# Two transformer layers in f32 on one core: values and first queries/keys as seven block products, and another pacing of the filling work

## The chip, the cores and the metric

The kernel runs on one core of a Trainium2 chip, as one launch. The metric is the device time of the launch in microseconds, the median of several runs. All arithmetic is f32.

## The reference

Two layers, each with a normalisation, causal attention with 16 heads of 32, and a gated feed-forward branch beside it. Tokens: 2 batches of 1024, width 512.

```python
xn = _layernorm(x, axis=-1)
x = x + _L0_attn_ref(xn, Wq, Wk, Wv, Wo) + _L0_ffn_ref(xn, w_gate, w_up, w_down)
xn = _layernorm(x, axis=-1)
x = x + _L1_attn_ref(xn, ...) + _L1_ffn_ref(xn, ..., gate_s, up_s, down_s)
# attention: Q, K, V = xn @ W.T; rotary turn of Q and K; causal softmax(Q K / sqrt(32)) V; @ Wo.T
# feed-forward: (silu(xn @ gate.T) * (xn @ up.T)) @ down.T; hidden width 2048, then 1408
# (in layer 1 gate, up and down have a scale per output)
```

The change concerns `V = xn @ Wv.T` and the Q and K of the first four heads.

## The kernel before, in words

**Phases.** A phase is one layer for one batch: (0, 0), (0, 1), (1, 0), (1, 1). The normalised input is held transposed in `xnT[ph, 0]` and `xnT[ph, 1]`, the first and the second 512 tokens, each 128 partitions by 4 chunks of the width by 512 tokens. For seven-product forms `ln_sums` (L561) and `ln_last_sum` (L572) make sums of blocks of it (`xs`, three tiles, and the last one in place in `xnT[ph, 1]`) on POOL.

**Units.** A `Unit` (L591) multiplies two weight blocks with both halves of the input in seven products instead of eight (Winograd's form of Strassen's method): four methods, `first` (L664) to `fourth` (L698), with 4, 4, 4 and 2 matmuls of 512 columns; the running sums stay in two PSUM banks (x and y; a third bank z is short-lived). `needs` (L654) lists what a method reads, for the planner. `sums` (L614) and `more_sums` (L626) make the sums of weight blocks on POOL, one unit ahead; in the first batch of a layer they are stored in DRAM, in the second they are loaded. `Hidden` (L944) is the unit of one 128-wide slice of gate and up, `QueriesKeys` (L763) that of a group of four heads' queries and keys. The queries and keys of a phase's first group, however, are four plain projections by `project_qk` (L752), 4 matmuls each, and the values are four calls of `project_v` (L812), 8 matmuls each (a shared partial sum in place of full products).

**Steps.** The attention of a phase is 40 steps (4 groups of heads, each with query blocks of 1, 2, 3 and 4 steps). In a step the main loop (L1462 and after) issues the scores of one step, the softmax pieces of earlier ones, and, LAG = 5 steps later, `weighted` (the product with the values) and at a block's end `total` and `normalise`. Between scores and `weighted` a `Fill` (L1207) puts other matmuls: units from a list `main`, the down projections `downs` (with additions onto x by DVE), output projections `outs`, further units of queries and keys `qk` that are due at a step, `values`, and `timed` items (loads, statistics of the next normalisation, `scale_down`, L890, which scales layer 1's down weights into DRAM during phase 0). `choose` (L1299) takes the next item; where a planned wait of `main` exceeds a bound, it takes a down projection. How much goes into a step is set by

```python
share = fill.left((ph + 1) * per_phase) / (end - i)
goal = share + max(-4.0, min(4.0, carried))
```

(L1508), in units of one matmul of 512 columns: what is left in the phase over the steps that are left. The last phase has LAG steps more, without scores.

**The end of a phase.** `queue_phase` (L1354) puts the next phase's transposes (8 tiles, one after the other) at the end of `main`; `project_qk` stands after the transposes 4 (k, first half), 5 (q, first half) and 7 (k and q, second half), and the first hidden unit of the next phase after them. The next phase's scores start when all four are done.

**Order.** The program's instructions aren't issued as they are written: `Schedule` (L152 and after) records them with modelled costs. PE keeps its recorded order; the other engines' orders are chosen by due times in `again` (L340).

**Buffers that matter.** `tmp`, tag "xs": two buffers of 128 x 512, used for raw inputs of the normalisation and by `scale_down`. `t5_p`: four buffers for copies out of PSUM. Three PSUM banks serve all filling work.

Of the kernel before, what the change touches and what calls it, by code (L numbers as in the profile page):

```python
# [40 lines left out]
def ts(n, size):  # L41
    return slice(n * size, (n + 1) * size)
# [364 lines left out]
def two_layers(ctx: ExitStack, tc: tile.TileContext, x_in, attn_w, ffn_w, ffn_s, rope, out):  # L407
# [48 lines left out]
    def let_go(name):  # L456
        bank_held[bank_of.pop(name)] = False
# [131 lines left out]
        nc.sync.dma_start(out=w[:, 2:4, :], in_=src[D // 2 :, :].rearrange("(c p) e -> p c e", p=P))  # L589

    class Unit:  # L591

# [46 lines left out]
        def product(self, bank, a, b, start=False):  # L639
            for c in range(2):  # L640
# [6 lines left out]
                    skip_group_check=True,  # L647
                )

        def scale(self):  # L650

            return None

        def needs(self, kind):  # L654

            if kind == "second":
                return [self.one, self.s12]
            if kind == "third":
                return [self.u, self.p5, self.s4]
            if kind == "fourth":  # L660
                return [self.p5]
            return []

        def first(self):  # L664
            self.begin()
            a, _ = self.weights()
            x0 = xnT[self.ph, 0]
            self.x = bank(f"ux{self.name}", hold=True)
            self.product(self.x, a[:, 0:2], x0[:, 0:2], start=True)
            one = self.one = keep(self.x, f"p1{self.name}")  # L670
            z = bank(f"uz{self.name}")
            self.product(z, a[:, 2:4], x0[:, 2:4], start=True)
            self.c11(z, one)

        def second(self):
            t1, t2, _ = xs[self.ph]
            self.product(self.x, self.s12[:, 1], t2)
            self.u = keep(self.x, f"u{self.name}")
            self.y = bank(f"uy{self.name}", hold=True)
            self.product(self.y, self.s12[:, 0], t1, start=True)  # L680
            self.p5 = keep(self.y, f"p5{self.name}", self.scale())

        def third(self, nxt):
            _, b = self.weights()
            x1 = xnT[self.ph, 1]
            self.product(self.x, b[:, 0:2], x1[:, 0:2])
            if nxt:
                nxt.sums()
            if self.scale() is None:
                nc.vector.tensor_tensor(self.p5, self.x, self.p5, ALU.add)  # L690
            else:
                nc.vector.scalar_tensor_tensor(self.p5, self.x, self.scale(), self.p5, ALU.mult, ALU.add)
            self.c22(self.p5)
            self.product(self.y, self.s4, x1[:, 2:4])
            let_go(f"uy{self.name}")
            self.c12(self.y, self.u)

        def fourth(self, nxt):  # L698
            _, b = self.weights()
            self.product(self.x, b[:, 2:4], xs[self.ph][2])  # L700
            let_go(f"ux{self.name}")
            if nxt:
                nxt.more_sums()
            self.c21(self.x)

    def keep(bank, name, scale=None):
        t = t5_p.tile([P, TB], F32, tag="t5", name=name)
        if scale is None:
            nc.scalar.copy(t, bank)
        else:  # L710
            nc.scalar.activation(t, bank, AF.Copy, scale=scale)
        return t
# [50 lines left out]
    class QueriesKeys(Unit):  # L763
# [8 lines left out]
        def begin(self):  # L772
            pass
# [5 lines left out]
        def c22(self, k1):  # L779
            rotated(self.ph, self.g, "k", 1, k1)  # L780

        def c12(self, bank, u):
# [26 lines left out]
        wv[ph] = wv_p.tile([P, DC, D], F32, tag="wv", name=f"wv{ph}")  # L809
        nc.sync.dma_start(out=wv[ph], in_=attn_w[layer][2].rearrange("(c p) e -> p c e", p=P))  # L810

    def project_v(ph, t):  # L812


        x0, x1, t1 = xnT[ph, 0], xnT[ph, 1], xs[ph][0]
        cols = ts(t, P)

        def product(bank, a, c0, start):
            for c in range(2):
                nc.tensor.matmul(  # L820
                    bank,
                    a[:, c, cols],
                    wv[ph][:, c0 + c, :],
                    start=(start and c == 0),
                    stop=(c == 1),
                    skip_group_check=True,
                )

        ps0 = bank(f"ps_v{ph}_{t}", hold=True)
        product(ps0, x0[:, 0:2], 0, True)  # L830
        both = keep(ps0, f"vv{ph}_{t}")
        ps1 = bank(f"ps_w{ph}_{t}")
        product(ps1, t1, 0, True)
        product(ps1, x1[:, 2:4], 2, False)
        for n in (0, 4):
            v[ph, t + n] = xp.tile([P, D], F32, tag=f"v{t + n}", name=f"v{ph}_{t + n}")
        nc.vector.tensor_tensor(v[ph, t + 4], ps1, both, ALU.add)
        product(ps0, x0[:, 2:4], 2, False)
        let_go(f"ps_v{ph}_{t}")
        nc.scalar.copy(v[ph, t], ps0)  # L840
        if t == QC // 2 - 1 and ph + 1 < len(phases):
            load_wv(ph + 1)

    parts = {}

# [98 lines left out]
    class Hidden(Unit):  # L944
# [19 lines left out]
        def c11(self, bank, one):  # L964
            nc.vector.tensor_tensor(self.h[0], bank, one, ALU.add)

        def c22(self, up):
            self.up = up

        def c12(self, bank, u):  # L970
            nc.vector.tensor_tensor(self.h[1], bank, u, ALU.add)
# [235 lines left out]
    class Fill:  # L1207
# [2 lines left out]


        def __init__(self):
            self.timed, self.main, self.downs, self.outs, self.qk, self.values = [], [], [], [], [], []

            self.later = 0.0
            self.turn = False
            self.unit = None
# [15 lines left out]
            self.main[at:at] = items  # L1233

        def left(self, end):
            n = 8.0 * len(self.values) + sum(item[0] for item in self.main) + self.later
            n += sum(len(d[2]) for d in self.downs) + 14.0 * len(self.qk)
            return n + sum(1.0 for o in self.outs if o[0] < end)

# [39 lines left out]
                    return o  # L1279
            return None  # L1280

        def do_values(self):
            self.values.pop(0)[2]()
            self.turn = False
            return 8.0

        def do_output(self, o):
            self.outs.remove(o)
            output_alone(*o[1:])
# [64 lines left out]
    def queue_phase(ph):  # L1354
# [236 lines left out]
```

## Time and profile before

| what | value |
|---|---|
| median of 3 runs | 1867.2 us (1863.83 to 1868.71) |
| the profiled execution's own time | 1868.41 us |
| its span | 1866.6 us |
| mean granted clock of TensorE | 0.997 |
| ACT, POOL busy share | 56%, 63% |

Each line of a profile gives an engine and an instruction's group. PE is TensorE's matmuls, PEld its weight loads (which run beside), DVE VectorE, ACT ScalarE, POOL GpSimd, SP the queue of most DMAs. A group line names output and inputs, tile form and count, then busy time and the mean of one, then idle time before it and what ended it. All instructions have one line number, 265, that of the helper that issues them, so they are told apart by tile: `sc` scores, `av` the product with the values, `ux`, `uy`, `uz` the banks of units (`ux_qk` and so on those of queries and keys), `d` down and output projections, `ps_o` output projections alone, `ps_v`, `ps_w` the values, `ps_k`, `ps_q` the plain projections, `tr` transposes of the normalised input, `mtr` those of softmax maxima. A timeline line is start, length, engine, instruction and count; what stands in brackets is an idle time and its releaser. A line of a busy table is a stretch, then for PE, PEld, DVE, ACT and POOL busy time and instructions, the granted clock, and the DMA share and rate.

### The profile page before, as it was taken

What the parts mean: (1) busy time and instruction counts of PE and PEld (TensorE: products, weight loads), DVE (VectorE), ACT (ScalarE), POOL (GpSimd) and SP (SyncE); (2) the same over time, 40 slices, a digit from 0 to 9 for tenths busy, and PEclk for the clock granted to TensorE, in tenths of its full rate; (3) what the DMA queues carried; (4) which work ended last, traced back from release to release, by engine and by line L of the source; (5) the groups of instructions that cost most, each with busy time, mean ns of one, the idle gap of its engine ahead of it and who ended that gap; (6) DMA issues with size and microseconds to landing.
All of it is one profiled execution on the core that took longest, in us unless ns stands there. A gap on an engine that the chain in (4) does not pass through costs nothing.

```text
span 1866.6 us, 25444 instructions
## 1 busy us (share of the span) xinstructions
PE 1838.2 (98%) x9180; PEld 838.8 (45%) x9180; DVE 1408.2 (75%) x1958; ACT 1038.8 (56%) x1243; POOL 1179.8 (63%) x1124
## 2 busy tenths in 40 slices
PE   7999999999999999999999999999999999999997
PEld 3444444444444444444444444444444444444443
DVE  3577866758778577587587786978879887989787
ACT  3465554546557464445375645665665665666661
POOL 5575856756567355373356875878758766766664
PEclk9999999999999999999999999999999999999998
DMA  5544222222243222222223323222222312221111
GB/s 197 161 140 140 83 65 68 85 66 83 68 136 108 94 80 63 68 79 81 68 82 102 119 85 129 64 74 73 80 83 88 124 35 91 72 69 52 57 39 67
DMA packets 139726, 164.21 MB, mean 88 GB/s; under 512 B 13264, under 2 KB 93136, under 8 KB 139600
## 3 DMA queue, kind: packets, MB, share of 16 engines
q1 hardware_dynamic: 139600, 162.58, 27.5%
q8 instruction: 73, 1.20, 0.3%
q14 instruction: 53, 0.43, 0.1%
HBM read 134.23 MB, written 28.31 MB: 87 GB/s over the span
## 4 chain that ended last, share of the span: by engine, by line
PE 88%; DVE 5%; DMA 3%; POOL 2%; ACT 1%; issue 1%; SPq 0%; POOLq 0%; DVEq 0%; ACTq 0%
PE d L265 23%; PE ux L265 18%; PE uy L265 8%; PE av L265 8%; PE sc L265 8%; PE uz L265 4%; PE ux_qk L265 4%; PE ps_w L265 3%; PE ps_v L265 3%; DVE s L265 2%; PE uy_qk L265 2%; PE ps_k L265 2%; PE ps_o L265 1%; PE ps_q L265 1%; DMA mb<-md 1%
## 5 line engine op out<-in xcount | busy, mean ns | idle before, releaser
L265 DVE TENSOR_TENSOR s<-s,mb 128x1024 f32<-128x1024 f32 (+2 forms) x448 | 492.1, 1132 | 24.7 <-DMA mb<-md 24.7
L265 POOL TENSOR_TENSOR acc<-acc,s 128x512 f32<-128x512 f32 (+1 forms) x384 | 478.1, 1270 | 39.5 <-ACT s L265 38.0
L265 ACT ACTIVATE s<-s 128x1024 f32<-128x1024 f32 (+1 forms) x320 | 305.3, 971 | 182.0 <-DVE s L265 179.7
L265 DVE TRANSPOSE_TENSOR_REDUCE rmax<-s 128x32 f32<-128x1024 f32 (+1 forms) x320 | 350.9, 1118 | 72.5 <-POOL s L265 42.1
L265 PE MATMUL d<-wd,hT 128*128 128x512 f32 x864 | 401.0, 597 | 0.4 <-ACT xnT L265 0.2
L265 ACT ACTIVATE s<-sc 128x1024 f32<-128x1024 f32 (+1 forms) x320 | 282.9, 933 | 207.9 <-PE sc L265 204.0
L265 POOL TENSOR_TENSOR acc<-s 128x512 f32<-128x512 f32 (+1 forms) x128 | 153.6, 1214 | 235.4 <-PE av L265 173.2
L265 PEld LDWEIGHTS d<-wd,hT 128*128 128x128 f32 x864 | 162.8, 191 | 201.1 <-issue 187.3
L265 DVE TENSOR_TENSOR x<-d,x 128x512 f32<-128x512 f32 x224 | 151.7, 678 | 93.1 <-PE d L265 92.1
L265 ACT ACT_TABLE_LOAD x160 | 205.3, 1283 | 10.9 <-DVE s L265 8.1
L265 PE MATMUL av<-s,v 128*32 128x256 f32 (+1 forms) x2560 | 159.7, 365 | 3.0 <-ACT s L265 2.0
L265 PEld LDWEIGHTS av<-s,v 128*32 128x32 f32 x2560 | 66.9, 109 | 148.7 <-issue 105.0
L265 POOL TENSOR_SCALAR_AFFINE_SELECT s<-s 128x512 f32<-128x512 f32 x128 | 89.9, 716 | 66.6 <-ACT s L265 64.9
L265 POOL TENSOR_TENSOR hT<-p,hT 128x512 f32<-128x512 f32 x53 | 75.8, 1430 | 75.2 <-ACT hT L265 75.2
L265 PE MATMUL ux<-xs,wu 128*128 128x512 f32 x212 | 100.8, 598 | 3.1 <-DVE p L265 3.1
L265 PE MATMUL ux<-xnT,wu 128*128 128x512 f32 x212 | 101.5, 601 | 0.0
L265 PE MATMUL ux<-xs,ws 128*128 128x512 f32 x212 | 101.0, 599 | 0.0
L265 PE MATMUL ux<-xnT,wg 128*128 128x512 f32 x212 | 101.0, 599 | 0.0
L265 PE MATMUL uy<-xnT,ws 128*128 128x512 f32 x212 | 99.7, 593 | 0.0
L265 PE MATMUL uz<-xnT,wg 128*128 128x512 f32 x212 | 99.6, 592 | 0.0
L265 PE MATMUL uy<-xs,ws 128*128 128x512 f32 x212 | 99.6, 592 | 0.0
L265 PE MATMUL d<-wo,oT 128*128 128x512 f32 x192 | 99.3, 599 | 0.1
(158 smaller groups left out, 2412.7 us busy)
## 6 DMA issues: line engine op xcount, KB each, us to landing
mb<-md SPq DMA_DIRECT2D x64, 512.0 KB, 3.7
wg<-in_gate SPq DMA_DIRECT2D x54, 256.0 KB, 2.8
wd<-in_down SPq DMA_DIRECT2D x32, 256.0 KB, 3.0
xr<-xm SPq DMA_DIRECT2D x32, 256.0 KB, 3.1
wu<-in_up SPq DMA_DIRECT2D x28, 256.0 KB, 2.9
s12gu<-ws SPq DMA_DIRECT2D x26, 256.0 KB, 2.0
ws<-s12gu SPq DMA_DIRECT2D x26, 256.0 KB, 2.6
wd<-wds SPq DMA_DIRECT2D x22, 256.0 KB, 2.9
```

The lines of the kernel that those rows point to most:

```text
L265: target(*[get(a) for a in args], **{k: get(a) for k, a in kwargs.items()})
```

## The change

- `project_v` goes; a class `Values(Unit)` computes the values by the four methods of a unit. The weight is cut into quarters (halves of the contraction by halves of the outputs), and a unit covers two tiles of 128 tokens in each half of the input (`pair` 0 or 1), so a phase has two. A product is four matmuls of 256 columns into the two halves of a bank. Sums of quarters, shared by both units, are made on POOL: s1 and s2 in the two "xs" buffers, s4 in a buffer of its own, the fourth in place in the weight.
- The values become `qk` items that are due at steps 3 and 4 of a phase and don't begin before steps 4 and 5 (`begins`).
- The first queries and keys of phases 1 to 3 become a `QueriesKeys` unit after all eight transposes. Phase 0's stay as they were.
- `c22` does the addition onto `p5` itself (the same instruction as before for `Hidden` and `QueriesKeys`); `needs` lists the input's sums as well.
- `scale_down` moves from steps 4 to 14 to steps 9 to 17 of phase 0.
- A step's share is weighted: 1.2 in the first ten steps of a phase, 1.5 in the last six of the program, 1 elsewhere.

```diff
--- before.py
+++ after.py
...
+        def blocks(self):
+            a, b = self.weights()
+            return (a[:, 0:2], a[:, 2:4], b[:, 0:2], b[:, 2:4]), (self.s12[:, 0], self.s12[:, 1]), self.s4
...
         def needs(self, kind):
             if kind == "second":
-                return [self.one, self.s12]
+                return [self.one, *self.sums_in(), *xs[self.ph]]
             if kind == "third":
-                return [self.u, self.p5, self.s4]
+                return [self.u, self.p5, self.s4, xnT[self.ph, 1]]
...
         def first(self):
             self.begin()
-            a, _ = self.weights()
+            a11, a12 = self.first_blocks()
...
-            self.product(self.x, a[:, 0:2], x0[:, 0:2], start=True)
+            self.product(self.x, a11, x0[:, 0:2], start=True)
...
-            self.product(z, a[:, 2:4], x0[:, 2:4], start=True)
+            self.product(z, a12, x0[:, 2:4], start=True)
             self.c11(z, one)
...
         def second(self):
...
-            self.product(self.x, self.s12[:, 1], t2)
+            _, (s1, s2), _ = self.blocks()
+            self.product(self.x, s2, t2)
...
-            self.product(self.y, self.s12[:, 0], t1, start=True)
...
         def third(self, nxt):
-            _, b = self.weights()
+            (_, _, s3, _), _, s4 = self.blocks()
...
-            self.product(self.x, b[:, 0:2], x1[:, 0:2])
+            self.product(self.x, s3, x1[:, 0:2])
...
-            if self.scale() is None:
-                nc.vector.tensor_tensor(self.p5, self.x, self.p5, ALU.add)
-            else:
-                nc.vector.scalar_tensor_tensor(self.p5, self.x, self.scale(), self.p5, ALU.mult, ALU.add)
-            self.c22(self.p5)
-            self.product(self.y, self.s4, x1[:, 2:4])
+            self.c22(self.x, self.p5)
+            self.product(self.y, s4, x1[:, 2:4])
...
         def fourth(self, nxt):
-            _, b = self.weights()
-            self.product(self.x, b[:, 2:4], xs[self.ph][2])
+            (_, _, _, a22), _, _ = self.blocks()
+            self.product(self.x, a22, xs[self.ph][2])
...
@@ -809,37 +821,85 @@
...
-    def project_v(ph, t):
-
-
-        x0, x1, t1 = xnT[ph, 0], xnT[ph, 1], xs[ph][0]
...
-        ps0 = bank(f"ps_v{ph}_{t}", hold=True)
-        product(ps0, x0[:, 0:2], 0, True)
-        both = keep(ps0, f"vv{ph}_{t}")
-        ps1 = bank(f"ps_w{ph}_{t}")
-        product(ps1, t1, 0, True)
-        product(ps1, x1[:, 2:4], 2, False)
-        for n in (0, 4):
-            v[ph, t + n] = xp.tile([P, D], F32, tag=f"v{t + n}", name=f"v{ph}_{t + n}")
-        nc.vector.tensor_tensor(v[ph, t + 4], ps1, both, ALU.add)
-        product(ps0, x0[:, 2:4], 2, False)
-        let_go(f"ps_v{ph}_{t}")
-        nc.scalar.copy(v[ph, t], ps0)
-        if t == QC // 2 - 1 and ph + 1 < len(phases):
-            load_wv(ph + 1)
+    class Values(Unit):
...
+        HALF = D // 2
+        shared = {}
+        def __init__(self, ph, pair, begins):
+            self.ph, self.pair, self.name, self.begins = ph, pair, f"_v{ph}_{pair}", begins
+        def quarter(self, c, r):
+            return wv[self.ph][:, 2 * c : 2 * c + 2, r * self.HALF : (r + 1) * self.HALF]
+        def first_blocks(self):
+            return self.quarter(0, 0), self.quarter(1, 0)
+        def blocks(self):
+            s1, s2, s4 = self.shared[self.ph]
+            a = self.quarter(0, 0), self.quarter(1, 0), self.quarter(0, 1), self.quarter(1, 1)
+            return a, (s1, s2), s4
+        def sums(self):
+            if self.ph in self.shared:
+                return
+            a11, a21, a22 = self.quarter(0, 0), self.quarter(0, 1), self.quarter(1, 1)
+            s1, s2 = (tmp.tile([P, 2, self.HALF], F32, tag="xs", name=f"s{n}_v{self.ph}") for n in (1, 2))
+            s4 = ws_p.tile([P, 2, self.HALF], F32, tag="wv4", name=f"s4_v{self.ph}")
+            self.shared[self.ph] = s1, s2, s4
+            nc.gpsimd.tensor_tensor(s1, a21, a22, ALU.add)
+            nc.gpsimd.tensor_tensor(s2, s1, a11, ALU.subtract)
+        def sums_in(self):
+            return list(self.shared[self.ph][:2])
+        def more_sums(self):
+            s1, s2, self.s4 = self.shared[self.ph]
+            if self.pair == 0:
+                nc.gpsimd.tensor_tensor(self.s4, self.quarter(1, 0), s2, ALU.subtract)
+                a21 = self.quarter(0, 1)
+                nc.gpsimd.tensor_tensor(a21, self.quarter(0, 0), a21, ALU.subtract)
+        def product(self, bank, a, b, start=False):
+            for n in range(2):
+                for c in range(2):
+                    nc.tensor.matmul(
+                        bank[:, n * self.HALF : (n + 1) * self.HALF],
+                        b[:, c, ts(2 * self.pair + n, P)],
+                        a[:, c, :],
+                        start=(start and n == 0 and c == 0),
+                        stop=(c == 1),
+                        skip_group_check=True,
+                    )
+        def begin(self):
+            self.v = [xp.tile([P, 2, D], F32, tag=f"v{self.pair}{n}", name=f"v{self.ph}_{self.pair}{n}") for n in range(2)]
+        def part(self, n, r):
+            return self.v[n][:, :, r * self.HALF : (r + 1) * self.HALF]
+        def pair_of(self, t):
+            return t.rearrange("p (n e) -> p n e", n=2)
+        def c11(self, bank, one):
+            nc.vector.tensor_tensor(self.part(0, 0), self.pair_of(bank), self.pair_of(one), ALU.add)
+        def c22(self, bank, p5):
+            nc.vector.tensor_tensor(self.part(1, 1), self.pair_of(bank), self.pair_of(p5), ALU.add)
+        def c12(self, bank, u):
+            nc.vector.tensor_tensor(self.part(1, 0), self.pair_of(bank), self.pair_of(u), ALU.add)
+        def c21(self, bank):
+            nc.scalar.copy(self.part(0, 1), self.pair_of(bank))
+            for n in range(2):
+                for i in range(2):
+                    v[self.ph, 4 * n + 2 * self.pair + i] = self.v[n][:, i, :]
+            if self.pair == 1 and self.ph + 1 < len(phases):
+                load_wv(self.ph + 1)
...
@@ -964,8 +1024,12 @@
...
-        def c22(self, up):
+        def c22(self, bank, up):
             self.up = up
+            if self.scale() is None:
+                nc.vector.tensor_tensor(up, bank, up, ALU.add)
+            else:
+                nc.vector.scalar_tensor_tensor(up, bank, self.scale(), up, ALU.mult, ALU.add)
...
         def left(self, end):
-            n = 8.0 * len(self.values) + sum(item[0] for item in self.main) + self.later
+            n = sum(item[0] for item in self.main) + self.later
...
         def choose(self, step):
             main = self.main[0] if self.main else None
-            v = self.values[0] if self.values and self.values[0][0] <= step else None
-            if main and main[2] in ("third", "fourth"):
-                v = None
-            if v and v[1] <= step:
-                return self.do_values, 8.0
...
+            full = full or (main and main[2] == "first" and getattr(main[3], "begins", 0) > step)
...
-            if v:
-                return self.do_values, 8.0
...
-        for t in range(QC // 2):
-
-            fill.values.append((t0 + (4, 4, 5, 5)[t] if ph else 0, t0 + (4, 4, 6, 6)[t], lambda t=t: project_v(ph, t)))
+        for pair in range(2):
+            begins = t0 + 4 + pair
+            fill.qk.append((begins - 1, Values(ph, pair, begins)))
+        fill.qk.sort(key=lambda x: x[0])
         if ph == 0:
             for k in range(HIDDEN[1]):
-                fill.at(t0 + 4 + k, lambda k=k: scale_down(k))
+                fill.at(t0 + 9 + 3 * k // 4, lambda k=k: scale_down(k))
...
@@ -1419,9 +1474,8 @@
...
-            for w in {4: "k", 5: "q", 7: "kq"}.get(t, ""):
-                fill.add(PROJ, lambda w=w, half=t // 6: project_qk(nxt, w, half), "other", lambda half=t // 6: [xnT[nxt, half]])
         fill.add(0.0, lambda: (ln_last_sum(nxt), marks.append(nxt)))
+        fill.add_unit(QueriesKeys(nxt, 0, 0), slices[0])
         fill.add_unit(units[nxt, 0], slices[0] + 1)
...
@@ -1457,6 +1511,13 @@
...
     total = len(steps)
+    def weight(i):
+        if i >= total + LAG - 6:
+            return 1.5
+        return 1.2 if i % per_phase < 10 else 1.0
...
         end = total + LAG if ph == len(phases) - 1 else (ph + 1) * per_phase
-        share = fill.left((ph + 1) * per_phase) / (end - i)
+        share = fill.left((ph + 1) * per_phase) * weight(i) / sum(weight(j) for j in range(i, end))
```

More of the change, by code (lines that the diff above doesn't have):

```diff
@@ L591, in two_layers @@
     class Unit:
+        s4 = None
         def kept(self):
@@ L665, in first @@
             self.begin()
-            a, _ = self.weights()
+            a11, a12 = self.first_blocks()
             x0 = xnT[self.ph, 0]
             self.x = bank(f"ux{self.name}", hold=True)
-            self.product(self.x, a[:, 0:2], x0[:, 0:2], start=True)
+            self.product(self.x, a11, x0[:, 0:2], start=True)
             one = self.one = keep(self.x, f"p1{self.name}")
             z = bank(f"uz{self.name}")
-            self.product(z, a[:, 2:4], x0[:, 2:4], start=True)
+            self.product(z, a12, x0[:, 2:4], start=True)
             self.c11(z, one)
+        def first_blocks(self):
+            a, _ = self.weights()
+            return a[:, 0:2], a[:, 2:4]
+        def sums_in(self):
+            return [self.s12]
         def second(self):
             t1, t2, _ = xs[self.ph]
-            self.product(self.x, self.s12[:, 1], t2)
+            _, (s1, s2), _ = self.blocks()
+            self.product(self.x, s2, t2)
             self.u = keep(self.x, f"u{self.name}")
             self.y = bank(f"uy{self.name}", hold=True)
-            self.product(self.y, self.s12[:, 0], t1, start=True)
+            self.product(self.y, s1, t1, start=True)
             self.p5 = keep(self.y, f"p5{self.name}", self.scale())
         def third(self, nxt):
-            _, b = self.weights()
+            (_, _, s3, _), _, s4 = self.blocks()
             x1 = xnT[self.ph, 1]
-            self.product(self.x, b[:, 0:2], x1[:, 0:2])
+            self.product(self.x, s3, x1[:, 0:2])
             if nxt:
                 nxt.sums()
-            if self.scale() is None:
-                nc.vector.tensor_tensor(self.p5, self.x, self.p5, ALU.add)
-            else:
-                nc.vector.scalar_tensor_tensor(self.p5, self.x, self.scale(), self.p5, ALU.mult, ALU.add)
-            self.c22(self.p5)
-            self.product(self.y, self.s4, x1[:, 2:4])
+            self.c22(self.x, self.p5)
+            self.product(self.y, s4, x1[:, 2:4])
             let_go(f"uy{self.name}")
@@ L777, in c11, with c22 @@
             rotated(self.ph, self.g, "q", 0, one)
-        def c22(self, k1):
+        def c22(self, bank, k1):
+            nc.vector.tensor_tensor(k1, bank, k1, ALU.add)
             rotated(self.ph, self.g, "k", 1, k1)
@@ L810, in load_wv, with first_blocks, sums_in @@
         nc.sync.dma_start(out=wv[ph], in_=attn_w[layer][2].rearrange("(c p) e -> p c e", p=P))
-    def project_v(ph, t):
-        x0, x1, t1 = xnT[ph, 0], xnT[ph, 1], xs[ph][0]
[L816 to L827, printed above, removed]
-        ps0 = bank(f"ps_v{ph}_{t}", hold=True)
-        product(ps0, x0[:, 0:2], 0, True)
-        both = keep(ps0, f"vv{ph}_{t}")
-        ps1 = bank(f"ps_w{ph}_{t}")
-        product(ps1, t1, 0, True)
-        product(ps1, x1[:, 2:4], 2, False)
-        for n in (0, 4):
-            v[ph, t + n] = xp.tile([P, D], F32, tag=f"v{t + n}", name=f"v{ph}_{t + n}")
-        nc.vector.tensor_tensor(v[ph, t + 4], ps1, both, ALU.add)
-        product(ps0, x0[:, 2:4], 2, False)
-        let_go(f"ps_v{ph}_{t}")
-        nc.scalar.copy(v[ph, t], ps0)
-        if t == QC // 2 - 1 and ph + 1 < len(phases):
-            load_wv(ph + 1)
+    class Values(Unit):
[5 more added lines that the diff above has]
+            return wv[self.ph][:, 2 * c : 2 * c + 2, r * self.HALF : (r + 1) * self.HALF]
+        def first_blocks(self):
+            return self.quarter(0, 0), self.quarter(1, 0)
[12 more added lines that the diff above has]
+            nc.gpsimd.tensor_tensor(s2, s1, a11, ALU.subtract)
+        def sums_in(self):
+            return list(self.shared[self.ph][:2])
[35 more added lines that the diff above has]
+                load_wv(self.ph + 1)
@@ L1212, in __init__ @@
         def __init__(self):
-            self.timed, self.main, self.downs, self.outs, self.qk, self.values = [], [], [], [], [], []
+            self.timed, self.main, self.downs, self.outs, self.qk = [], [], [], [], []
             self.later = 0.0
@@ L1280, in late_output @@
             return None
[L1282 to L1285, printed above, removed]
         def do_output(self, o):
```

## The prediction

> **What bounds the kernel now.** I read the page first (engine totals, slices), then PE's groups by form, then PE's timeline at four places, PE's waits, and the busy table of the last phase. The page:
>
> ```profile
> span 1866.6 us, 25444 instructions
> PE 1838.2 (98%) x9180; PEld 838.8 (45%) x9180; DVE 1408.2 (75%) x1958; ACT 1038.8 (56%) x1243; POOL 1179.8 (63%) x1124
> PE   7999999999999999999999999999999999999997
> ```
>
> PE is busy in 98% of the span and falls below nine tenths only in the first and the last slice. DVE, next at 75%, has slack. So a matmul taken out should shorten the span by what it takes in the stream. The groups' mean (about 597 ns) is the length of one record with its pipeline; the stream's pace is the distance between starts. PE's timeline in phase 0 shows it (start, length, count):
>
> ```profile
> 52.04 1.88 PE L265 MATMUL ps_v<-wv,xnT 128*128 128x512 f32 x4
> 53.75 1.88 PE L265 MATMUL ps_w<-wv,xs 128*128 128x512 f32 x4
> 55.47 1.88 PE L265 MATMUL ps_w<-wv,xnT 128*128 128x512 f32 x4
> ```
>
> Four records take 53.75 - 52.04 = 1.71 us, 0.429 each. The groups show two records for each matmul of the code (`project_v` issues 4 + 4 matmuls in 16 calls, 128 in all):
>
> ```profile
> L265 PE MATMUL ps_v<-wv,xnT 128*128 128x512 f32 x128 | 60.9, 601 | 0.0
> L265 PE MATMUL ps_w<-wv,xs 128*128 128x512 f32 x64 | 30.2, 594 | 0.3 <-DVE p_qk L265 0.3
> L265 PE MATMUL ps_w<-wv,xnT 128*128 128x512 f32 x64 | 30.1, 592 | 0.0
> ```
>
> 128 + 64 + 64 = 256 records. A matmul of 512 columns is therefore 2 x 0.429 = 0.858 us of PE's time.
>
> **Values, on the path.** Before: 32 matmuls per phase, 27.5 us. After: two units of 7 products, each product 2 x 2 matmuls of 256 columns, 56 matmuls per phase, 112 records. No full-array record of 256 columns is in the trace. If it takes half of 0.429, the phase costs 112 x 0.2145 = 24.0 us: 3.43 us less, 13.7 us in four phases. The bounds: from below half, as a record streams its columns. From above, the question is whether a weight load per 256 columns stays hidden. The nearest rows are the transposes, a fresh load for every 128 columns, and a pair of loads of the f32 kind (PE, then PEld):
>
> ```profile
> 508.61 0.60 PE L265 MATMUL tr<-ident,xr 128*128 128x128 f32 x4
> 508.94 0.30 PEld L265 LDWEIGHTS ps_o<-wo,oT 128*128 128x128 f32 x2
> ```
>
> Four transposes in 0.60 us, one being 0.273 long (their group's mean, 277 ns), start (0.60 - 0.273) / 3 = 0.109 us apart, a quarter of 0.429: a load per 128 columns did not slow that stream. Two f32 loads of 0.19 each end within 0.30, so 0.11 apart. By the transposes a 256-column record is 0.218, which takes 448 x 0.0035 = 1.6 us off the gain. The upper end is a load that shows: a group of four right after scores is 1.98 long where one in the stream is 1.88 ("98.70 1.88" against "48.50 1.98" in the timeline), so 0.10 for each load not hidden, at worst its whole 0.19. That is 45 to 85 us over 448 records. I take half price, since transposes are the nearest row, and keep the upper end as a rival.
>
> The Trainium skill, "TensorE: Matmul & The Clock Gate", section "Back-to-back issue gap", speaks against this split: sustained pairs of load and matmul measured 131 ns at 512 columns but 81 ns at 128, so the price does not fall with the columns. Interpolated between them (an estimate), 256 columns would be 0.75 of 512; 448 records would then cost 448 x 0.75 x 0.429 = 144 us against 110 before, 34 us more instead of 13.7 less. The transposes here show a price that is proportional, so I do not follow it.
>
> **First queries and keys, on the path.** `project_qk` did 4 x 4 matmuls at each start; `QueriesKeys(nxt, 0, 0)` does 14 in phases 1 to 3 (phase 0 keeps the old form). 3 x 2 x 0.858 = 5.1 us less. Together with the values: **-18.9 us**.
>
> **The other engines, beside it.** Values: DVE 6 additions from PSUM instead of 4 per phase (0.69 us each: +1.4), ACT 8 copies as before, POOL 4 new sums of 512 columns (a pair of such, xnT<-xnT, took 2.49 us: +5.0). Queries and keys: DVE +3 additions (2.1 us), POOL +4 sums of 256 columns at 0.73 (2.9 us) in phases 1 and 2. Phase 2 also stores three sums, and phase 3 loads them, on SP's queue (alike: ws<-s12gu, 2.6 us to landing). Per phase of 370 to 500 us that is under 2% of any engine, hidden under PE. If POOL were late, PE would wait in `second`; units already make their sums one unit (12 us) ahead. `scale_down` moves from steps 4 to 14 to steps 9 to 17, because s1 and s2 of the values now hold both "xs" buffers; each needs two loads, 1.27 us of POOL and one store, some 7 to 10 us apart before, so 11 fit into 8 steps of over 10 us. It is needed two phases later: nothing.
>
> **What is late next: the starts of phases.** The four projections stood between transposes 4 to 7 and after them; now the unit comes after all eight. At 508.61 the last tile is transposed, copied by 510.2, and POOL ended its xs sums at 515.9 behind other work. `first` needs only the first half's xnT (3.4 us), `second` needs xs (2.3 us short), `third` needs the last sum on xnT (2.5 us on POOL, under `second`). Downs and outputs can fill: at 510.28, 512.10, 527.47 and 532.00 PE still had some. The first scores of the phase need keys of half 0, which now come out of the last product; from there copy, shuffle, two multiplications and an addition are about 0.6 + 0.7 + 0.8 + 1.7 + 1.3 = 5 us, under the hidden unit that follows (14 x 0.858 = 12 us). Bounds 0 to 12 us for each of three starts (the second half of the transposes without cover: 3.1 for a load, 0.8, 0.6, 0.6, twice, and the 2.3); I take 0.7 each, **+2 us**, since downs were left over.
>
> **The end.** PE's timeline of the last steps, and the busy table:
>
> ```profile
> 1822.37 0.27 PE L265 MATMUL mtr<-ident,m 128*32 128x128 f32 x1 [0.88 <-DVE m L265]
> ...
> 1828.71 0.62 PE L265 MATMUL av<-s,v 128*32 128x256 f32 x4 [1.44 <-ACT s L265]
> 1829.91 1.49 PE L265 MATMUL av<-s,v 128*32 128x256 f32 x12 [0.57 <-ACT s L265]
> 1834.04 1.93 PE L265 MATMUL av<-acc,ones 128*32 128x256 f32 x8 [2.64 <-POOL acc L265]
> 1835.91 7.42 PE L265 MATMUL d<-wd,hT 128*128 128x512 f32 x12
> ```
>
> ```profile
> 1530.00:1570.00 40.00, 39.89 (x218) 18.16 (x217) 26.14 (x40) 23.94 (x29) 17.77 (x19) 1.00 0.31 100
> 1690.00:1730.00 40.00, 40.00 (x252) 18.59 (x251) 37.96 (x57) 22.62 (x27) 28.59 (x27) 1.00 0.12 40
> 1810.00:1840.00 30.00, 24.47 (x130) 9.74 (x129) 26.76 (x35) 12.27 (x13) 24.79 (x19) 0.83 0.11 36
> ```
>
> PE waits 0.88 + 1.44 + 0.57 + 2.64 = 5.5 us for the last softmaxes. After those waits the granted clock halves (0.83 over 30 us is 10.2 us at a half): twelve records take 7.42 us instead of 12 x 0.429 + 0.17 = 5.3, the eight of `total` 1.93 instead of 0.61 as elsewhere, the av group some 0.7 more: 4.1 us. Together 9.6 us. The last phase's planned work is about 10 units x 14 + 88 + 42 + 28 + 32 = 330; before, 334 / 45 steps = 7.4 each; after, weights sum to 12 + 29 + 9 = 50, so the last six steps get 1.5 x 6.6 = 9.9. That is 2.5 x 0.858 = 2.1 us more per step, 13 us beside the 9.6. But the chain behind the waits (DVE 26.76 of 30 busy) is not shortened. Bounds 0 to 9.6; I take **-6 us**. The tail after the last `total` stays.
>
> The middle of the last phase pays: 6.6 instead of 7.4 per step makes steps 8% shorter, where DVE was 85% busy (236.7 of 280 us from 1530 to 1810), so about 91%. Where DVE stood at 92% (1490 to 1530) PE sat idle 1.1 us of 40; over 280 us that would be 7.7. Bounds 0 to 7.7; I take **+1.5**, since at 37.96 of 40 (1690) PE lost nothing. The weight of 1.2 at other starts moves matmuls between full stretches: nothing.
>
> **Sum.** -18.9 + 2 - 6 + 1.5 = -21.4 us. The profiled execution took 1868.4 us (span 1866.6 and 1.8 around it), so 1847.0; it lay 1.2 above the median of the runs, 1867.2, so 1845.8 there: 1846.
>
> **Rivals.** (1) *The gain is spent at the starts of phases*: without four projections as filler, transposes and sums stand bare, 4 us at each of three starts instead of 0.7, or values that begin no earlier than step 4 leave a step without work. Sum -11.4, so 1856. For it: POOL is 10.00 of 10 busy from 497 to 507. Against: downs and outputs were left. (2) *The end does not mend*, being bound by DVE's chain, and the shorter steps cost 4: -18.9 + 2 + 4 = -13, so 1854. For it: DVE's 26.76 of 30. (3) *Slower: the weight load of the 256-column records shows.* Price 0.10 each, 448 x 0.10 = 45 us, sum +23.6, so 1891. It decides from 21.4 / 448 = 0.048 us per record, that is at a pace over 0.262 instead of 0.2145. Against: the transposes' 0.109. For: f32 loads are 0.19 long, nearly 0.2145. (4) *The change doesn't do what it says*: stalls move and eat the products' gain, within 0.3%.
>
> **How the numbers follow.** Forecast 0.64 at 1846; rival 1 0.15, rival 2 0.13, rival 3 0.05, rival 4 0.03. Low end: -18.9 - 9.6 with no costs gives 1838.7, say 1838; high end takes in rivals 1 and 2, up to 1858. Within 0.3% (5.6 us, about what measurement tells from no change) is above 1861.6: faster 0.92, same 0.03, slower 0.05.
>
> **What would show it.** Records of the values' products starting 0.215 us apart (right) or over 0.26 (rival 3); 9180 - 256 + 448 - 96 + 84 = 9360 matmul records, PE's busy time down; no half clock and under 4 us of waits in the last 47 us; in PE's waits, no row on xs, xnT or tr above some 2 us at the three starts.

## The result and the profile after

The changed kernel takes 1857.1 us (median of 6; before 1867.2): 10.1 us less, ratio 0.9946 with an interval of 0.9931 to 0.9962. The forecast was 21 us less, 1846. The page of the changed kernel:

```profile
span 1859.1 us, 25872 instructions
PE 1825.3 (98%) x9360; PEld 875.9 (47%) x9360; DVE 1422.7 (77%) x1973; ACT 1044.7 (56%) x1247; POOL 1206.3 (65%) x1148
PE   7999999999999999999999999999999999999999
```

The count of 9360 is the one forecast, and the last slice is full now. PE's timeline at the first values (start, length, instruction, count):

```profile
97.84 1.99 PE L265 MATMUL ux_v<-wv,xnT 128*128 128x256 f32 x8
99.67 1.89 PE L265 MATMUL uz_v<-wv,xnT 128*128 128x256 f32 x8
...
103.11 1.89 PE L265 MATMUL ux_v<-s_v,xs 128*128 128x256 f32 x8
104.84 1.89 PE L265 MATMUL uy_v<-s_v,xs 128*128 128x256 f32 x8
```

Eight records of 256 columns take 104.84 - 103.11 = 1.73 us, 0.216 each, with a fresh weight load each: half of 0.429 to within 2 ns. Rival 3 is out. The price that the Trainium skill gives in "TensorE: Matmul & The Clock Gate", section "Back-to-back issue gap" (131 ns at 512 columns, 81 at 128), does not hold for this f32 stream.

The trace above is of an execution of 1860.9 us, the slowest of its six. A second trace of the same kernel took 1856.1, and I read the waits there. For all traces I took the distance between the starts of two neighbouring records on PE. Its usual value is the median, over all traces, for two records of the same forms at the same place of their run; what exceeds it by more than 12 ns I call a wait (a half clock counts as waiting too), and the rest is the stream. By this, versions with the same matmuls have streams within 1.1 us of each other. The expectations quote waits from an earlier working of the same kind, which differ from these by up to some 2 us. A step "p.n" is step n of phase p and begins with its scores. Before against after (second trace), with the prediction's terms:

| term | before | after | change | forecast |
|---|---|---|---|---|
| stream | 1810.6 | 1791.4 | -19.2 | -18.9 |
| steps 30 to 39 of phases 0 to 2 (transposes, queries and keys) | 4.3 | 7.2 | +2.9 | +2 |
| 3.38 to the end | 11.2 | 4.4 | -6.8 | -6 |
| 3.10 to 3.37 | 3.8 | 3.4 | -0.4 | +1.5 |
| first ten steps of the four phases | 8.8 | 17.2 | +8.4 | 0 |
| of these, phase 3 | 4.3 | 13.7 | +9.4 | 0 |
| steps 10 to 29 of phases 0 to 2 | 7.4 | 9.4 | +2.0 | 0 |
| ahead of the first scores | 7.5 | 8.3 | +0.8 | 0 |
| sum | 1853.6 | 1841.3 | -12.3 | -21.4 |

So the four terms I had priced came out at -23.5, and the stretches I had priced at nothing gave 11.2 back. The time ahead of the first scores is the same code in all kernels and varies from 5.8 to 9.1 between traces. PE's timeline of the end shows the mended part (weights alone and the changed kernel have the same counts there; this is the kernel with the weights alone):

```profile
1799.83 0.63 PE L265 MATMUL av<-acc,ones 128*32 128x256 f32 x4 [0.78 <-POOL acc L265]
1802.17 0.62 PE L265 MATMUL av<-acc,ones 128*32 128x256 f32 x4 [1.71 <-POOL acc L265]
...
1819.04 7.13 PE L265 MATMUL d<-wd,hT 128*128 128x512 f32 x16
```

Of the four waits of 5.5 us two of 2.5 are left (0.78 and 1.72 in the changed kernel's second trace), and sixteen records take 7.13 us, so the clock is whole.

The lost part, at the turn from phase 2 to 3. Before:

```profile
1439.05 1.15 PE L265 MATMUL sc<-q_1T,k_3T 32*128 32x256 f32 x16
...
1441.09 1.88 PE L265 MATMUL ux<-xnT,wg 128*128 128x512 f32 x4
...
1449.74 1.99 PE L265 MATMUL uy<-xnT,ws 128*128 128x512 f32 x4
1451.66 1.07 PE L265 MATMUL av<-s,v 128*32 128x256 f32 x16
1452.66 0.94 PE L265 MATMUL sc<-q_1T,k_3T 32*128 32x256 f32 x16
...
1466.19 0.86 PE L265 MATMUL av<-s,v 128*32 128x256 f32 x16
1466.87 0.61 PE L265 MATMUL av<-acc,ones 128*32 128x256 f32 x8
```

After (second trace):

```profile
1439.12 1.15 PE L265 MATMUL sc<-q_1T,k_3T 32*128 32x256 f32 x16
1440.20 1.98 PE L265 MATMUL ux<-xs,wu 128*128 128x512 f32 x4
1442.87 1.07 PE L265 MATMUL av<-s,v 128*32 128x256 f32 x16 [0.69 <-DVE oT L265]
1443.87 0.94 PE L265 MATMUL sc<-q_1T,k_3T 32*128 32x256 f32 x16
1444.74 1.98 PE L265 MATMUL ps_o<-wo,oT 128*128 128x512 f32 x4
...
1455.69 0.63 PE L265 MATMUL av<-s,v 128*32 128x256 f32 x4
1457.43 0.62 PE L265 MATMUL av<-s,v 128*32 128x256 f32 x8 [1.11 <-ACT s L265]
...
1459.57 1.07 PE L265 MATMUL av<-acc,ones 128*32 128x256 f32 x4 [1.29 <-POOL rmax L265]
```

Steps 2.38 and 2.39 hold two matmuls each (before 13 and 4) and last 4.8 and 3.8 us (13.6 and 5.5). The softmax of step 2.35 must be done when PE reaches `weighted` in step 3.00; from the scores of 2.38 that was 1466.2 - 1439.1 = 27.1 us before and is 1455.7 - 1439.1 = 16.6 now, so PE waits 1.11 us for ACT and 1.29 for POOL. Values, turning of queries and keys and softmax meet in 3.04 and 3.05, and POOL's sums end last:

```profile
1505.18 0.63 PE L265 MATMUL av<-acc,ones 128*32 128x256 f32 x4 [1.87 <-POOL acc L265]
1506.05 0.63 PE L265 MATMUL av<-acc,ones 128*32 128x256 f32 x4 [0.24 <-POOL acc L265]
1506.61 1.26 PE L265 MATMUL sc<-q_1T,k_0T 32*128 32x256 f32 x16
1507.80 3.31 PE L265 MATMUL ux_v<-wv,xnT 128*128 128x256 f32 x8
```

The eight records after them take 3.31 us instead of 1.99: the granted clock is 0.50 from 1507.1 to 1510.5.

### The profile page after: what moved, and what is told of

Same layout as the page of the kernel before. It is cut to its first block, busy times and chain, and to the rows that moved or that the text cites. A ratio compares the mean times of both kernels' runs of the same rounds, so it can differ in the third digit from the quotient of the medians.

```text
span 1859.1 us, 25872 instructions
## 1 busy us (share of the span) xinstructions
PE 1825.3 (98%) x9360; PEld 875.9 (47%) x9360; DVE 1422.7 (77%) x1973; ACT 1044.7 (56%) x1247; POOL 1206.3 (65%) x1148
## 4 chain that ended last, share of the span: by engine, by line
PE 89%; DVE 5%; DMA 2%; POOL 2%; ACT 1%; issue 1%; SPq 0%; POOLq 0%; ACTq 0%; DVEq 0%
PE d L265 23%; PE ux L265 18%; PE uy L265 9%; PE av L265 9%; PE sc L265 8%; PE ux_qk L265 5%; PE uz L265 4%; PE ux_v L265 3%; PE uy_qk L265 2%; DVE s L265 1%; PE uy_v L265 1%; PE uz_qk L265 1%; PE ps_o L265 1%; POOL acc L265 1%; DVE rmax L265 1%
## 5 line engine op out<-in xcount | busy, mean ns | idle before, releaser
L265 DVE TENSOR_TENSOR s<-s,mb 128x1024 f32<-128x1024 f32 (+2 forms) x448 | 498.3, 1141 | 20.4 <-DMA mb<-md 20.3
L265 POOL TENSOR_TENSOR acc<-s 128x512 f32<-128x512 f32 (+1 forms) x128 | 157.9, 1248 | 190.0 <-PE av L265 115.1
L265 DVE TENSOR_TENSOR x<-d,x 128x512 f32<-128x512 f32 x224 | 152.0, 680 | 99.8 <-PE d L265 99.7
L265 ACT ACT_TABLE_LOAD x164 | 210.4, 1283 | 11.2 <-DVE s L265 8.3
L265 POOL TENSOR_SCALAR_AFFINE_SELECT s<-s 128x512 f32<-128x512 f32 x128 | 97.4, 776 | 92.9 <-ACT s L265 91.5
L265 PE MATMUL uy<-xnT,ws 128*128 128x512 f32 x212 | 99.7, 593 | 0.4 <-ACT p L265 0.4
```

The costliest lines, as they stand in the source:

```text
L265: target(*[get(a) for a in args], **{k: get(a) for k, a in kwargs.items()})
```

## The experiments

All times are medians; each ratio is to runs of the kernel before on the same chip. The four groups and the changed kernel's first runs were not all on one chip, so between groups the ratios compare better than the times.

**1. The parts.** No weights (1 in all steps); on the kernel before, the weights alone; on the kernel before, the `QueriesKeys` unit at three starts alone; values alone (the changed kernel without weights and with the old projections, whose edit this is).

```diff
-        fill.add_unit(QueriesKeys(nxt, 0, 0), slices[0])
+            for w in {4: "k", 5: "q", 7: "kq"}.get(t, ""):
+                fill.add(PROJ, lambda w=w, half=t // 6: project_qk(nxt, w, half), "other", ...)
```

No weights: 1859.9, ratio 0.9970 (0.9958 to 0.9981).

> The changed kernel with the weights of the steps all at 1. Theory A (each part does its own work; the weights mend the end by some 6 us and cost the middle): about 4 to 6 us slower than the changed kernel, so some 1862 us, with the waits and the half clock of the last 47 us back at 9 to 10 us. Theory B (the new waits come from the crowded first steps that the weight of 1.2 makes): faster than the changed kernel, 1850 to 1854, with the two waits at the start of the last phase gone. Theory C (an edit of the plan re-deals waits at places of no relation to it): within 5 us of the changed kernel either way, with waits at other places in the traces.

Weights alone: 1856.0, 0.9947 (0.9934 to 0.9960).

> The kernel before with the weights alone. A: 1861 us (6 less than before), end waits from 9.6 to about 3 us, rest as before. B: 1867 to 1872, the end mended and new waits at the first steps of the phases. C: 1862 to 1872, waits at scattered places, PE's matmul time unchanged.

Queries and keys alone: 1867.1, 1.0003 (0.9994 to 1.0012).

> The kernel before with the first queries and keys of phases 1 to 3 as seven products, values and pacing as before. By the products alone: 5.1 us less, 1862. A: 1862 to 1864 (0.7 us of waits at each of three starts). Rival of the prediction (no filler between the last transposes): 1867 or more, with waits on tr, xs or xnT of some 2 to 4 us at each start. C: 1858 to 1868.

Values alone: 1857.2, 0.9957 (0.9942 to 0.9972).

> The changed kernel with four plain projections at each start as before and no weights: the values (and the later scaling of the down weights) alone. By the products: 13.7 us less, 1853.5. A: 1853 to 1856. If less matmul work leaves the other engines too little time anywhere (theory D, the waits grow wherever PE's time shrinks): 1858 to 1862, with more small waits everywhere. C: 1850 to 1860.

The streams are 1791.8, 1810.4, 1805.4 and 1797.4 us against 1810.6: products save what they should wherever they stand (values 13.2, queries and keys 5.2, both 18.8). Without weights the end keeps its waits (9.9 to 11.4), with the weights alone it has 4.4. The weights bring more than the end's 6: 9.8 us. Queries and keys alone bring nothing: waits rise from 43.1 to 48.5, of which 6.4 instead of 3.0 stand in 3.04 to 3.09. Values alone bring 8 us of their 13; they too wait 7.2 us in 3.04 to 3.09. B fell (no weights is slower). A held for the end, not for queries and keys, and for the values in part.

**2. Two parts together.** Values and weights; queries and keys with weights; the late weight (below) in phases 0 to 2; the end's weight alone.

```diff
+        if i % per_phase >= per_phase - 2 and i < total - per_phase:
+            return 2.0
         return 1.2 if i % per_phase < 10 else 1.0
```

Values and weights: 1847.4, 0.9897 (0.9884 to 0.9909).

> The changed kernel with the four plain projections at each start in place of the seven-product unit: values and weights. Theory E (the unit of queries and keys uses up the phase's other work early and leaves the last two steps of phase 2 with 2 matmuls each, where the softmax then falls behind and PE waits in the first steps of phase 3; the weights and the values each keep their own gain): 1847 to 1850, under 1 us of waits in steps 0 and 1 of phase 3, against 5.3 in the changed kernel. Theory C (every edit re-deals waits without a rule): 1850 to 1858. Theory D (waits grow wherever PE's time shrinks): some 1855, since 13.7 us less matmul work are taken back as in the values alone.

Queries and keys with weights: 1859.6, 0.9958 (0.9943 to 0.9973).

> The kernel before with the seven-product unit at three starts and the weights, values as before. Its plan too has 2 and 2 matmuls in the last two steps of phase 2. E: waits of 3 to 6 us at the first steps of phase 3 take the products' 5 us back: 1854 to 1858. By the products alone (1856.0 of the weights alone, less 5.1): 1851. C: 1850 to 1860.

Late weight: 1846.0, 0.9879 (0.9865 to 0.9893).

> The changed kernel with a weight of 2 in the last two steps of phases 0 to 2, so that the last two steps of phase 2 hold 13 and 8 matmuls instead of 2 and 2; the plan of phase 3 holds the same counts, step by step, as the changed kernel's. E: the waits and the half clock at steps 0 and 1 of phase 3 (5.3 us) go: 1851 to 1853, or less if waits in phases 0 and 1 go too. C: within 4 us of 1857 either way, waits elsewhere. If the waits there come from the sums and the turning of queries and keys on POOL and DVE and not from the bare steps, they stay: 1857.

The end's weight alone: 1858.0, 0.9955 (0.9943 to 0.9967).

> The changed kernel with the weight of 1.5 at the end and 1 at the first steps of phases. If the end is what the weights mend (my prediction's step): 1853, 7 us less than without weights (1859.9) and 4 less than the changed kernel. If the first steps' weight works too (the weights alone gave 9.8 us, more than the 6 of the end): 1856 to 1860, slower than or equal to the changed kernel, with waits back at steps 0 to 11 of the phases.

Values and weights add up: 0.43% and 0.53% alone, 1.03% together; phase 3's first ten steps wait 4.6 us, no clock is halved in the trace. Theory D falls. Adding the unit of queries and keys to this makes the changed kernel: 0.9897 becomes 0.9946, some 9 us slower, though it takes matmuls out. Added to the weights alone it does not bring its 5 us either (0.9947 and 0.9958, whose intervals overlap): there the waits at 3.00 and 3.01 that I expected were small (1.4 with 3.02 and 3.03), though the last two steps of phase 2 hold 2 and 2, and those from 3.04 to 3.09 were 5.9 us instead of 2.2. The late weight, with every product and unit in place, is 11 us faster than the changed kernel, more than theory E had forecast.

**3. One place at a time.** A weight of 1.75 in the last two steps of phase 2 alone (10 and 8 matmuls there; the counts of the other phases unchanged); phase 3's value units due a step later (3.03 holds 6 instead of 2, the first ten steps 88 instead of 80); both; and the kernel before with a weight of 0.3 there (0 and 2 instead of 13 and 4).

```diff
+        if 2 * per_phase + 38 <= i <= 2 * per_phase + 39:
+            return 1.75
-            fill.qk.append((begins - 1, Values(ph, pair, begins)))
+            fill.qk.append((begins - (ph < 3), Values(ph, pair, begins)))
```

Phase 2's end filled: 1857.5, 0.9944 (0.9932 to 0.9956).

> The changed kernel with a weight of 1.75 in the last two steps of phase 2 alone. The plan's counts of phases 0, 1 and 3 are the changed kernel's, step by step; phase 2 ends with 10 and 8 matmuls instead of 2 and 2. Theory E (bare steps): the 5.3 us of waits and half clock in steps 0 and 1 of phase 3 fall under 1, 1850 to 1853. If the earlier late weight's gain came from phases 0 and 1: 1856 to 1858.

Values later: 1857.7, 0.9950 (0.9938 to 0.9962).

> The changed kernel with the two value units of phase 3 due one step later, so that step 3 of phase 3 holds 6 matmuls instead of 2; phases 0 to 2 have the changed kernel's counts, 2 and 2 at the end of phase 2 included. E: the waits at steps 0 and 1 stay (5 us), those at steps 4 and 5 (5.6 us) fall by 3 to 5: 1852 to 1855. Theory C: any time from 1850 to 1862, the waits at steps 0 and 1 changing too.

Both: 1853.4, 0.9923 (0.9910 to 0.9935).

> The two edits together: phase 2 ends with 10 and 8, step 3 of phase 3 holds 6. E: both stretches under 2 us of waits, 1846 to 1849, the sum of the two gains. If a wait that goes merely comes back later in the phase: no better than the better of the two.

The kernel before, made bare: 1870.2, 1.0015 (1.0006 to 1.0023).

> The kernel before, its products and its projections unchanged, with a weight of 0.3 in the last two steps of phase 2: they hold 0 and 2 matmuls instead of 13 and 4, and phase 3 has the same counts as before. E: the bare steps alone bring waits of 4 to 6 us with a half clock at steps 0 and 1 of phase 3: 1870 to 1873. If the seven-product unit's own work on POOL and DVE is what makes those waits: 1866 to 1868, as before.

Place by place, waits do as E says: filled, steps 3.00 to 3.03 wait 1.2 us instead of 6.6; later values cut 3.04 to 3.09 from 7.1 to 2.4. But the time follows only when both are done, and then by 3 to 4 us, at the edge of what the intervals tell: with phase 2 filled, 7.3 us remain in 3.04 to 3.09, and with both, phase 3 waits 6.1 instead of 1.7 in steps 10 to 29.

These three versions hold one caution. Filled, phase 3's first ten steps take 99.7 us against 104.2 in the changed kernel's second trace, but phase 0 takes 495.8 against 492.3, though PE, ACT, DVE and POOL have the same instructions in the same order up to 500 us. The traces of the two other edits of the changed kernel show the same there (496.2 and 496.6). Nearly all of the difference arises at step 0.17, in the wait for ACT shown in the last section. So a part of what the edits gained was lost, in these traces, where they changed nothing. No run of the changed kernel on that chip is on record; what filling alone is worth in time stays open.

In the kernel before, bare steps cost 2.6 us. That time lies in E's range, but the waits at 3.00 and 3.01, 2.1 us, do not reach the 4 to 6 expected. So bare steps do cost time; by themselves they do not bring the whole loss.

**4. Which phase.** The changed kernel again; the late weight of 2 in phase 0, in phase 1, in both, and in phases 1 and 2; last, values and weights without the unit of queries and keys, with 1.75 in phases 1 and 2.

Again: 1856.3, 0.9944 (0.9932 to 0.9956).

> The changed kernel once more, for a second trace and more times: its first trace was the slowest of its six executions. If the waits named so far (steps 0 and 1 and 4 and 5 of phase 3, 7 of phase 1, the end) are the kernel's own, they stand at the same steps, within 1 us each; those that are not there were chance. Time 1855 to 1859.

Phase 0: 1857.7, 0.9948 (0.9935 to 0.9960).

> The weight of 2 in the last two steps of phase 0 alone. By the traces phase 0 gets no shorter (waits 13.8 against 8.7): 1857 to 1861. If the sum is what counts and not the place of each wait, 1850 to 1855.

Phase 1: 1856.7, 0.9938 (0.9925 to 0.9951).

> The weight of 2 in the last two steps of phase 1 alone. By the traces, the late weight's phase 1 was 5 us shorter than the changed kernel's (waits 4.1 against 9.3) and its phase 0 no shorter: 1851 to 1854. If it does nothing by itself: 1857.

Phases 0 and 1: 1854.4, 0.9929 (0.9915 to 0.9943).

> The weight of 2 in the last two steps of phases 0 and 1 alone; phase 2 ends with 2 and 2 matmuls as in the changed kernel, and phase 3 has its counts. If the bare steps of phase 2 hold the missing time: 1853 to 1857, with the 5 us at steps 0 and 1 of phase 3 there. If it lies in phases 0 and 1 (their shares at the starts being lower when more is left for the end): 1847 to 1850, though the bare steps stay.

Phases 1 and 2: 1845.7, 0.9879 (0.9866 to 0.9893).

> The changed kernel with the weight of 2 in the last two steps of phases 1 and 2. The plan's counts in phases 1 to 3 are those of the late weight in all three phases (1846), those of phase 0 the changed kernel's. If the plan of phase 2 and the start of phase 3 hold the gain: 1844 to 1849. If the late weight's 1846 needed phase 0 as well: 1851 to 1857.

Values and weights, filled: 1853.3, 0.9926 (0.9912 to 0.9939).

> Values and weights with the old projections (1847.4 before) and a weight of 1.75 in the last two steps of phases 1 and 2, which then hold 9 and 8 matmuls instead of 4 and 4 in phase 2. If fuller last steps help by themselves: 1843 to 1846. If they only help where the steps were bare (4 and 4 did not make PE wait at steps 0 and 1: 1.3 us): 1846 to 1849.

In the second trace of the changed kernel, the waits of phase 3 stand at the same steps with the same lengths (1.87 us at 3.04, 0.78 and 1.72 at 3.38, 1.11 and 1.29 at 3.00 against 1.87, 0.77 and 1.71, 1.10 and 1.30 in the first): they are the plan's, not chance. Others come and go: 1.42 us at 1.35 stands in the first trace alone, 0.61 at 3.05 in the second. The half clock varies too: 17.1 us of it in the first trace, 6.8 in the second.

The late weight in phase 0 or in phase 1 changes nothing clear; in both it gives 1854.4, still with 12.7 us of waits in phase 3's first ten steps. In phases 1 and 2 it is as fast as in all three (ratio 0.9879 both), the fastest versions. The weight of 2 in phase 2 alone was not run, only 1.75, so what phase 1 adds is open. The turn from phase 2 to 3 with phases 1 and 2 weighted late:

```profile
1420.26 1.15 PE L265 MATMUL sc<-q_1T,k_3T 32*128 32x256 f32 x16
1421.34 1.12 PE L265 MATMUL ps_o<-wo,oT 128*128 128x512 f32 x2
...
1430.88 1.88 PE L265 MATMUL uy<-xs,ws 128*128 128x512 f32 x4
1432.69 1.07 PE L265 MATMUL av<-s,v 128*32 128x256 f32 x16
...
1450.77 0.86 PE L265 MATMUL av<-s,v 128*32 128x256 f32 x16
1451.45 0.61 PE L265 MATMUL av<-acc,ones 128*32 128x256 f32 x8
```

30.5 us from the scores of 2.38 to the `weighted` of 3.00, and no wait. Phase 3's first ten steps wait 4.3 us in all, as before the change, with the same counts there as in the changed kernel (13.7). Against the changed kernel's second trace its stream is 0.6 us longer and its waits 13.1 shorter, of which 9.4 lie there. The starts of the scores say the same without any usual distance: from 3.00 to 3.10, with the same 80 matmuls, the five traces with bare last steps in phase 2 take 103.0 to 107.2 us, the two with 13 and 8 matmuls there 95.1 and 95.3.

The filled version of values and weights is the counterexample: 9 and 8 instead of 4 and 4 made it some 5 us slower by the ratios (0.9897 to 0.9926), with 8.2 us of waits in 3.04 to 3.09 instead of 3.3. Fuller last steps are no rule.

## Why the prediction was wrong

- *Products, -18.9*: right: -19.2, at 0.216 us a record. The streams of the other versions agree (values 13.2, queries and keys 5.2).
- *The end, -6*: right, -6.8.
- *The middle of the last phase, +1.5*: nothing (-0.4), the lower end of its bounds.
- *The starts of phases, +2, "since downs were left over"*: this is the step that failed. The waits in steps 30 to 39 were +2.9, near enough. But the unit of queries and keys cost 9 us net (values and weights against the changed kernel) instead of bringing 5.1 - 2 = 3.1. I looked at what PE had to do while the unit runs, around 510 to 532 us in phase 0, and not at what the steps after it are left with, which I priced at nothing. Of phases 0 to 2 the last has the least other work, and its last two steps kept 2 matmuls each. PE then waited for ACT and POOL in the steps 3.00 to 3.09: 13.7 us instead of 4.3, half clock included.
- *"The weight of 1.2 at other starts ... nothing"*: with the weights alone there were 1.4 and 1.7 us of waits in steps 10 to 29 of phases 0 and 2 instead of 3.0 and 3.1, so it seems to have helped there; it was tried apart only on the changed kernel (1858.0 without it), where no difference is clear.
- *Rival 1* came nearest, in time (1856) and in place, with the values' step without work (3.03). Its reason was half of it: transposes were not bare, the steps after them were. And giving 3.03 its work back did not change the time (1857.7), so the near hit in time is in part luck.

That another pacing alone regains the missing time is shown: the same products, units and sums took 1845.7 us with the last two steps of phases 1 and 2 weighted otherwise. That the unit's own DVE and POOL work must cost it is excluded by the same run, which has the unit in place. What stays open is a rule by which one could say, from a plan's counts, where waits will stand: filling the bare steps alone brought nothing clear in time, and in another version it did harm. POOL's sums for `total` ended PE's waits at 3.04 and 3.05 in all versions with a new unit but one, for 0.8 to 4.4 us in sum; in the kernel before, with the weights alone and with both edits no such wait was over 0.25 us. How far one plan gets POOL ahead of another was not tried by itself.

## What to carry to other kernels

Where one engine was 98% busy, a matmul taken out was gained only while the other engines kept their distance. So count, for the whole plan and not for the changed place alone, how many matmuls each step is left with and whether the five steps between a step's scores and its `weighted` leave the softmax its time. A part that saves work can cost more than it saves until the pacing is set again for it.

## What the runs showed of the hardware

Half the clock followed some waits of PE and not others, and no length of wait in these traces parts the two. At 3.38, 13 traces have the same two waits for POOL, 0.78 and 1.71 us to within 0.01; after them the granted clock was 0.50 for 3.4 us in 5 of these traces and 1.00 in 8. Longer waits show the same. One in phase 0, with the same instructions, in the first trace of the changed kernel:

```profile
267.52 1.95 PE L265 MATMUL ux<-xs,ws 128*128 128x512 f32 x4 [2.33 <-ACT p L265]
269.31 1.88 PE L265 MATMUL uy<-xs,ws 128*128 128x512 f32 x4
```

and in that with phase 2's end filled:

```profile
269.37 2.55 PE L265 MATMUL ux<-xs,ws 128*128 128x512 f32 x4 [2.57 <-ACT p L265]
271.72 3.02 PE L265 MATMUL uy<-xs,ws 128*128 128x512 f32 x4
```

Four records take 3.02 us instead of 1.88 after 2.57 us, and their usual time after 2.33; in the trace with both edits the clock halved after 2.19. Between the first scores and the last step the half clock came in stretches of 3.4, 6.8 and 10.2 us, 0 to 17.1 us per trace. The changed kernel's six runs spread over 7 us (1853.7 to 1860.9).
